# A two-layer hybrid block on one core: GpSimd's order of squares and rotation, four-step down-projections, and a shorter list ahead of the first scores

## The chip, the cores and the metric

The kernel runs on one core of a Trainium2 chip. The metric is device time in microseconds (us) of one execution, the median of several runs. The core has five engines with queues of their own, each of which works in order: TensorE (PE in the profile; its weight loads are PEld), VectorE (DVE), ScalarE (ACT), GpSimd (POOL) and SyncE (SP, which here only issues DMAs). GpSimd issues DMAs too. All DMAs run on 16 DMA engines.

## The reference

The input x is 4 x 1024 x 256 in float32. Four blocks are added to it one after the other, each on the layer norm of what stands there:

```
x = x + attention_a(norm(x));  x = x + ffn(norm(x))
x = x + attention_b(norm(x));  x = x + ffn(norm(x))
```

Both attentions have 16 heads of 64 and a full softmax over 1024 keys. Attention a makes queries, keys and values straight from the 256 columns. Attention b norms again (with scale and bias), projects down to 128 columns for queries and 128 for keys and values, projects up to heads, and rotates queries and keys: of each even and odd component e and o with the angle of the position,

```
rot = stack([e * cos - o * sin, e * sin + o * cos])
out = out @ w_out.T + residual
```

Its top-k indices are not part of the result. The ffn is 256 to 1024 and back, with a gelu.

## The kernel before, in words

All of x stays in SBUF as four tiles of 128 x 8 x 256, one a batch. Products are in float32.

*Attention.* Work goes by head pairs: for each of 4 batches 8 pairs of heads, 32 in all, which `attention` numbers g. For each head pair there are 8 steps, one for each block of 128 queries, 256 steps s in all. A step makes the scores of its queries for both heads (128 x 1024 each, `scores`, L214), their negative maximum on DVE (L224), the exponentials on ScalarE (L225), the inverted sums (`invert`), and a transpose of all probabilities on DVE within squares of 32 x 32 (`turn`, L244).

Two consecutive steps share a buffer T; here they are called a couple, numbered h. What DVE's transpose leaves undone, moving squares between groups of partitions, is done by 16 DMAs of 136 KB from T to pT (`send`, L261): SyncE issues eleven at the end of the couple's second step, GpSimd five in the step after. `weigh` multiplies the values by pT (av) in two halves, in steps 2h + 4 and 2h + 5; `divide` applies the sums (oT), and `project` multiplies by the output weights two steps later (po); ScalarE copies po to got, and GpSimd adds it to x (L292). T and pT have two buffers each, got one, the scores' PSUM three.

The order on every engine is written out by hand in `steps_with`, which is the order in the code: in step s come the inverted sums of s, the scores of s + 1 and the first exponentials, GpSimd's squares (even steps), `project` with its add, `weigh`, the second exponentials, `divide`, `turn`, SyncE's squares (odd steps), and last the pieces that are due in step s. Pieces are the preparation of a later head pair or batch; a dictionary keeps them by step, and those of one step run in the order in which they were put in.

*Preparation in layer B.* For head pair g, counted from step 8(g - 1): `qk(i, qb)` makes keys (i = 1) at -1 and 1 and queries (i = 0) at 3 and 5, for two blocks of 512 positions. It has ScalarE copy the product to `straight` (L596) and has GpSimd issue two DMAs of 128 KB that exchange even and odd partitions into `turned` (L598). One step later `rotate` runs three GpSimd operations (L603 to L605): straight times cosine, turned times sine (with the sign in the table), and the sum. Values come at 5 and 7. For a batch, `batch_b` standardizes its rows twice, adds to x on GpSimd (L551), transposes, and projects down (`down`, pc): both blocks for keys and values in step 3NT - 1 = 23 of the batch's count, both for queries in step 25. The first key product of the batch's first head pair falls in step 23 as well.

*Start.* What the first head pair of layer A needs stands in a list `first` and runs before step -1: the weight loads, standardization of both blocks of 512 rows with their statistics, transposes, two key products, two query products and four value products, in this order. For layer B the same list is worked off inside the first ffn's loop.

*ffn* runs between and after the attentions, its ends overlapped with their steps; the change leaves it alone but for the list just named.

Of the kernel before, what the change touches and what calls it, by code (L numbers as in the profile page):

```python
# [28 lines left out]
NHB = NT // HB  # L29
LAG = 4  # L30
NK = 2 * NT + 1
SENT = NG * HB * NK * SQ
POOL_DMA = 5
EPS = 1e-5
# [3 lines left out]
def hybrid_block_kernel(  # L38
# [98 lines left out]
    def standardize(dst, src, shift, rstd):  # L137
        nc.scalar.activation(dst, src, AF.Identity, scale=rstd, bias=shift)  # L138
# [24 lines left out]
    def attention(prep_batch, prep_pair, wo):  # L163
# [118 lines left out]
        def project(h):  # L282
            g, t0 = divmod(HB * h, NT)
            b, pr = pairs[g]
            po = ps_mm.tile([P, HB, D], F32, tag="mm", name="po")
            for t in range(HB):
                paired(po[:, t, :], [(oT[h][:, ts(t, P)], [wos[g]] * 2)])
            oT.pop(h)
            got = tmp.tile([P, HB, D], F32, tag="tmp", name="got")
            nc.scalar.copy(got, po)  # L290
            xd = xs[b][:, t0 : t0 + HB, :]
            nc.gpsimd.tensor_add(xd, xd, got)  # L292

        def steps_with(others):
            for k, f in others:
                pieces.setdefault(k, []).append(f)
            for s in range(-1, n + LAG + 1):
                h, part = divmod(s - LAG, HB)
                ahead = 0 <= s + 1 < n
                if 0 <= s < n:  # L300
                    invert(s)
                if ahead:
                    scores(s + 1)
                    exponentials(s + 1, 0)
                if part == 0 and 0 <= s // HB - 1 < n // HB:
                    send(s // HB - 1, nc.gpsimd, squares[len(squares) - POOL_DMA :])
                    T.pop(s // HB - 1)
                if part == 0 and 0 <= h - 1 < n // HB:
                    project(h - 1)
                if 0 <= h < n // HB:  # L310
                    weigh(h, part)
                if ahead:
                    exponentials(s + 1, 1)
                if part == 1 and 0 <= h < n // HB:
                    divide(h)
                if 0 <= s < n:
                    turn(s)
                if part == 1 and 0 <= s < n:
                    send(s // HB, nc.sync, squares[: len(squares) - POOL_DMA])
                for f in pieces.get(s, ()):  # L320
                    f()

        return first, steps_with
# [127 lines left out]
    def layer_a():  # L451
# [5 lines left out]
        def batch_a(b):  # L457
            work = []
            for qb in range(NQB):
                k = {}  # L460

                def straight(t, b=b, k=k, qb=qb):
                    if t == 0 and b == 0:
                        for i in range(TQ):
                            rows.measure(qb, i)
                        rows.finish[qb]()
                    if t == 0:
                        k["xn"] = xnp.tile([P, TQ, D], F32, tag="xn", name="xn")
                    standardize(
                        k["xn"][:, t, :], xs[b][:, qb * TQ + t, :],  # L470
                        *rows.factors(NQB * b + qb, t)[:2],
                    )

                def turned(c, b=b, k=k, qb=qb):
                    if c == 0:
                        p, tag = ((lowp, "low"), (highp, "high"))[qb]
                        hTs[b, qb] = p.tile([P, NC, QB], F32, tag=tag, name="hT")
                    transposed(hTs[b, qb], k["xn"], c)

                work += [(10 * qb + t, lambda t=t, f=straight: f(t)) for t in range(TQ)]  # L480
                work += [(10 * qb + 5 + 2 * c, lambda c=c, f=turned: f(c)) for c in range(NC)]
            return work
# [42 lines left out]
        later = [(4 + i, lambda i=i: rows.measure(2 + i // TQ, i % TQ)) for i in range(6 * TQ)]  # L525
        later += [(4 + 6 * TQ, lambda: rows.finish[2]())]
        first, steps = attention(batch_a, pair_a, wo_a)
        return first, lambda others: steps(later + others)


    def layer_b(rows):
# [4 lines left out]
        def batch_b(b):  # L536
            work = []
            for qb in range(NQB):
# [33 lines left out]
                work += [(10 * qb + t + 2, lambda t=t, f=second: f(t)) for t in range(TQ)]  # L572
                work += [(10 * qb + 7 + 2 * c, lambda c=c, f=turned: f(c)) for c in range(NC)]

                work += [(3 * NT + 1 - 2 * i, lambda i=i, f=down: f(i)) for i in range(2)]
            return work

        def pair_b(b, pr):
            made = {}

            def load():
                w = made["w"] = wp.tile([P, 3, NC, P], F32, tag="w", name="w")[:, :, 0, :]
                for i, up in enumerate((wuq, wuk, wuv)):
                    nc.gpsimd.dma_start(w[:, i], up[:, ts(pr, P)])

            def qk(i, qb):

                pq = ps_mm.tile([P, QB], F32, tag="mm", name="pq")
                paired(pq, [(made["w"][:, i, :], [cs[b, i][:, ts(qb, QB)]] * 2)])
                name = ("qT", "kT")[i]  # L590
                if qb == 0:
                    made[name] = qkp.tile([P, S], F32, tag=name, name=name)
                straight = made[name][:, ts(qb, QB)]
                turned = rp.tile([P, QB], F32, tag="turned", name="turned")
                made[i, qb] = straight, turned
                nc.scalar.mul(straight, pq, (scale_b, 1.0)[i])  # L596
                for r in range(2):
                    nc.gpsimd.dma_start(turned[r::2], straight[1 - r :: 2])  # L598

            def rotate(i, qb):  # L600

                straight, turned = made[i, qb]
                nc.gpsimd.tensor_mul(straight, straight, cos_sb[:, ts(qb, QB)])  # L603
                nc.gpsimd.tensor_mul(turned, turned, sin_sb[:, ts(qb, QB)])  # L604
                nc.gpsimd.tensor_add(straight, straight, turned)  # L605

            def values(qb):
                if qb == 0:
                    made["v"] = vp.tile([P, NT, P], F32, tag="v", name="v")
                pv = ps_mm.tile([P, TQ, P], F32, tag="mm", name="pv")  # L610
                for t in range(TQ):
                    lhsT = cs[b, 1][:, ts(qb * TQ + t, P)]
                    paired(pv[:, t, :], [(lhsT, [made["w"][:, 2, :]] * 2)])
                nc.scalar.copy(made["v"][:, ts(qb, TQ), :], pv)

            work = []
            for i in (1, 0):
                for qb in range(NQB):
                    k = 3 - 4 * i + 2 * qb
                    work += [(k, lambda i=i, qb=qb: qk(i, qb))]  # L620
                    work += [(k + 1, lambda i=i, qb=qb: rotate(i, qb))]
            work += [(5 + 2 * qb, lambda qb=qb: values(qb)) for qb in range(NQB)]
            return {name: lambda name=name: made[name] for name in ("qT", "kT", "v")}, load, work

# [21 lines left out]
def _rope_tables():  # L646
# [7 lines left out]
    sin = np.concatenate([np.sin(freqs), np.sin(freqs)], -1)[:, ::2]  # L654
    cos = np.repeat(cos.T, 2, axis=0)
    sin = np.repeat(sin.T, 2, axis=0)
    sin[0::2] *= -1.0
    return cos.astype(np.float32), sin.astype(np.float32)


# [40 lines left out]
```

## Time and profile before

| | us |
|---|---|
| three runs | 3381.72, 3386.45, 3389.66 |
| median | 3386.45 |
| profiled execution, its own time | 3386.3 |
| its span on the core | 3384.5 |
| PE busy in the span | 3253.2 (96%) |
| DVE busy | 2593.1 (77%) |
| ACT busy | 1902.1 (56%) |
| POOL busy | 1800.8 (53%) |
| first scores on PE | 27.85 |

The profile's page names groups of instructions as line, engine, operation, output<-inputs, with the count, the busy time and the mean of one, and the idle time of the engine before them with what ended it. A DMA's row on GpSimd or SyncE is the time of its issue; how long it took to land stands in a part of its own. The timeline merges neighbours of one kind ("x5") and gives start and duration. The stretches give the busy time of each engine between two times, and the share of their time that the 16 DMA engines moved data.

Layer A runs from about 28 to 1450 us, the ffn to 1750, layer B to 3150, and the second ffn to the end.

### The profile page before, as it was taken

The page shows a single profiled execution, that of the slowest core. Times are in us where ns is not written, and L with a number is a line of the kernel's source. Part 1 is how long each engine was busy: PE and PEld are TensorE (multiplying, and loading weights), DVE is VectorE, ACT ScalarE, POOL GpSimd, SP SyncE. Part 2 cuts the span into 40 slices and gives each one's busy share as a digit, 9 for nine tenths or more (in the row PEclk, how much of TensorE's full clock was granted, in tenths as well). Part 3 has the DMA queues.
Part 4 walks back from the last instruction along what each step waited for, and adds up shares of the span by engine and source line. Part 5 has one row for each costly group of instructions (what it writes and reads, how often), then busy time and mean ns, then how long its engine had stood idle before and what let it go on. Part 6 is the DMA issues. An engine that isn't in the chain of part 4 may idle for free.

```text
span 3384.5 us, 60980 instructions
## 1 busy us (share of the span) xinstructions
PE 3253.2 (96%) x20864; PEld 1679.4 (50%) x20864; DVE 2593.1 (77%) x2638; ACT 1902.1 (56%) x3667; POOL 1800.8 (53%) x2546
## 2 busy tenths in 40 slices
PE   7999999999999999999999999999999999999999
PEld 3445444544454444456554444444444444444566
DVE  6988888888888888951059998898889989999200
ACT  5566556655565555542445665566656655655332
POOL 3333334343333343330258887888788978886200
PEclk9999999999999999999999999999999999999999
DMA  7788788888887888840038888888888888888200
GB/s 211 204 210 208 205 214 212 211 208 214 210 210 206 214 214 210 210 115 3 6 105 233 227 239 226 237 246 231 224 236 243 242 225 239 243 235 228 61 19 19
DMA packets 229585, 647.36 MB, mean 191 GB/s; under 512 B 74304, under 2 KB 82496, under 8 KB 229280
## 3 DMA queue, kind: packets, MB, share of 16 engines
q1 hardware_dynamic: 143696, 400.74, 46.2%
q0 software_dynamic: 85584, 242.74, 25.2%
q8 instruction: 170, 2.79, 0.4%
q14 instruction: 135, 1.11, 0.1%
HBM read 35.00 MB, written 4.19 MB: 12 GB/s over the span
## 4 chain that ended last, share of the span: by engine, by line
PE 67%; DVE 11%; SPq 8%; DMA 6%; issue 4%; ACT 3%; POOL 1%; DVEq 0%; POOLq 0%; ACTq 0%
PE sc L214 19%; PE av L158 18%; SPq L261 8%; PE pq L158 8%; PE po L380 7%; PE ph L369 6%; DVE nmax L224 5%; DVE T L244 5%; DMA pT<-T 5%; PE po L158 4%; PE pv L158 4%; ACT p L225 1%; PE pc L158 1%; DMA turned<-qT 1%; DVE oT L275 1%
## 5 line engine op out<-in xcount | busy, mean ns | idle before, releaser
L225 ACT ACTIVATE p<-sc,nmax 128x1024 f32<-128x1024 f32 x1024 | 1143.8, 1117 | 729.5 <-DVE nmax L224 729.5
L224 DVE TENSOR_REDUCE nmax<-sc 128x1 f32<-128x1024 f32 x1024 | 1201.9, 1215 | 325.5 <-PE sc L214 324.9
L244 DVE STREAM_TRANSPOSE T<-p 128x2176 f32<-128x2176 f32 x512 | 1246.3, 2434 | 11.1 <-ACT p L233 3.9
L158 PE MATMUL av<-pT,v 128*64 128x256 f32 x8192 | 994.7, 385 | 79.4 <-DMA pT<-T 56.9
L214 PE MATMUL sc<-kT,qT 64*128 64x512 f32 x4096 | 1033.0, 617 | 7.2 <-ACT p L225 7.2
L261 POOL DMA_DIRECT2D pT<-T x1280 | 625.8, 496 | 777.9 <-issue 268.7
L158 PEld LDWEIGHTS av<-pT,v 128*64 128x64 f32 x8192 | 579.5, 137 | 542.9 <-issue 273.3
L214 PEld LDWEIGHTS sc<-kT,qT 64*128 64x128 f32 x4096 | 366.8, 187 | 483.9 <-issue 352.5
L292 POOL TENSOR_TENSOR x<-x,got 128x512 f32<-128x512 f32 x256 | 326.8, 1276 | 224.7 <-ACT got L290 220.4
L233 ACT COPY p<-total 128x128 f32<-128x128 f32 x512 | 152.0, 297 | 312.5 <-DVE total L232 312.4
L387 DVE TENSOR_TENSOR x<-x,po 128x512 f32<-128x512 f32 x32 | 21.9, 685 | 363.4 <-PE po L380 363.4
L158 PE MATMUL po<-wo,oT 128*64 128x256 f32 x2048 | 277.7, 392 | 0.4 <-DVE oT L275 0.4
L373 ACT ACTIVATE gT<-ph,b_sb 128x512 f32<-128x512 f32 x128 | 87.4, 685 | 305.4 <-PE ph L369 305.3
L158 PE MATMUL pq<-hT,w 128*64 128x512 f32 x1024 | 247.0, 605 | 5.1 <-DVE oT L275 4.0
L158 PEld LDWEIGHTS po<-wo,oT 128*64 128x64 f32 x2048 | 124.3, 136 | 230.2 <-issue 129.5
L380 PE MATMUL po<-w_sb,gT 128*128 128x256 f32 x1024 | 226.0, 381 | 6.2 <-ACT hT L147 6.2
L369 PE MATMUL ph<-hT,w_sb 128*128 128x512 f32 x512 | 228.9, 601 | 0.2 <-ACT hT L147 0.2
L380 PEld LDWEIGHTS po<-w_sb,gT 128*128 128x128 f32 x1024 | 193.5, 190 | 38.4 <-ACT hT L147 9.0
L225 ACT ACTIVATION_READ_ACCUMULATOR p<-sc,nmax 128x1 f32 x1024 | 201.4, 197 | 0.0
L355 POOL TENSOR_TENSOR x<-x,b_sb 128x256 f32<-128x256 f32 x64 | 44.5, 727 | 276.4 <-ACT xn L138 276.4
L604 POOL TENSOR_TENSOR turned<-turned,sin_sb 128x512 f32<-128x512 f32 x128 | 162.3, 1268 | 0.0
L369 PEld LDWEIGHTS ph<-hT,w_sb 128*128 128x128 f32 x512 | 97.0, 192 | 117.1 <-issue 111.3
(88 smaller groups left out, 2188.8 us busy)
## 6 DMA issues: line engine op xcount, KB each, us to landing
pT<-T SPq DMA_DIRECT2D x2816, 136.0 KB, 4.2
pT<-T POOLq DMA_DIRECT2D x1280, 136.0 KB, 4.7
turned<-kT POOLq DMA_DIRECT2D x128, 128.0 KB, 2.7
turned<-qT POOLq DMA_DIRECT2D x128, 128.0 KB, 3.0
w<-in_wqkv_a POOLq DMA_DIRECT2D x96, 128.0 KB, 4.9
wo<-in_wo_a POOLq DMA_DIRECT2D x32, 128.0 KB, 4.4
wo<-in_wo_b POOLq DMA_DIRECT2D x32, 128.0 KB, 3.4
out<-x SPq DMA_DIRECT2D x16, 256.0 KB, 2.1
```

Of the source, the lines that this page charges most:

```text
L158: nc.tensor.matmul(out[ts(j, DH)], lhsT[:, ts(j, DH)], rhs[j], start=(first and i == 0), stop=(last and i == len(parts) - 1),)
L214: nc.tensor.matmul(sc[s, j][:, ts(m, 512)], qT()[rows, ts(qs, P)], kT()[rows, ts(m, 512)], start=True, stop=True,)
L224: nc.vector.tensor_reduce(nmax, sc[s, j], AX.X, ALU.max, negate=True)
L225: nc.scalar.activation(probs[s][:, ts(j, NT)].rearrange("p k c i -> p (k c i)"), sc.pop((s, j)), AF.Exp, bias=nmax, accum_out=total[s][:, ...
L233: nc.scalar.copy(probs[s][:, 2 * NT].rearrange("p (j c) i -> p j (c i)", j=2), t.unsqueeze(2).to_broadcast([P, 2, DH]),)
L244: nc.vector.transpose(T[h][:, :, q, :, :].rearrange("p c k i -> p k c i"), probs.pop(s))
L261: engine.dma_start(pT[h][ts(c, SQ), a], T[h][ts(a, SQ), c])
L292: nc.gpsimd.tensor_add(xd, xd, got)
L369: nc.tensor.matmul(ph, w1_sb[:, c, ts(f, P)], hT[n][:, c, :], start=(c == 0), stop=(c == NC - 1),)
L373: nc.scalar.activation(gT[n][:, f, :], ph, AF.Gelu, bias=b1_sb[:, f : f + 1])
L380: nc.tensor.matmul(po[n][:, t % 2, :], gT[n][:, f, ts(t, P)], w2_sb[:, f, :], start=(f == 0), stop=(f == NF - 1),)
L604: nc.gpsimd.tensor_mul(turned, turned, sin_sb[:, ts(qb, QB)])
```

## The change

It has three parts.

*GpSimd's order in layer B.* `project` no longer adds to x; it returns the add, and `steps_with` calls it after the pieces of the step. A second list of pieces, at s + LATE = s + 0.5, follows the add. The rotation is cut in two: part 0 (at k + 1) multiplies the straight rows by the sine into `other` and exchanges even and odd partitions of that product by DMA; part 1 (at k + 1.5) multiplies by the cosine and adds. The exchange moves from `qk` in the odd step to the even step; its sine table has the sign in the other rows.

*Down-projections.* The four `down` of a batch fall in steps 23, 24, 26 and 28 of the batch's count, keys and values first.

*Start of layer A.* The list is put in a new order: statistics of block 0, its standardization, statistics of block 1, an Exp of one column on ScalarE (`ready`), transposes of block 0, keys of block 0, standardization of block 1 (now on VectorE) and its transposes, keys of block 1, queries of block 0. The queries of block 1 become a piece of step -1 and the values pieces of steps 0 and 1.

```diff
+LATE = 0.5
             xd = xs[b][:, t0 : t0 + HB, :]
-            nc.gpsimd.tensor_add(xd, xd, got)
+            return lambda: nc.gpsimd.tensor_add(xd, xd, got)
...
+                add = None
                 if part == 0 and 0 <= h - 1 < n // HB:
-                    project(h - 1)
+                    add = project(h - 1)
...
                 for f in pieces.get(s, ()):
+                    f()
+                if add:
+                    add()
+                for f in pieces.get(s + LATE, ()):
                     f()
...
-                    if t == 0 and b == 0:
-                        for i in range(TQ):
-                            rows.measure(qb, i)
-                        rows.finish[qb]()
...
+                    if b == 0 and qb == 1:
+                        nc.vector.tensor_scalar(dst, src, rstd, shift, op0=ALU.mult, op1=ALU.add)
+                    else:
+                        standardize(dst, src, shift, rstd)
...
+        loads, xn, pair = first[:2], first[2:14], first[14:]
+
+        def measured(qb):
+            for t in range(TQ):
+                rows.measure(qb, t)
+            rows.finish[qb]()
+
+        def ready():
+
+            nc.scalar.activation(small.tile([P, 1], F32, tag="nmax", name="ready"), eps, AF.Exp)
+
+
+        first = loads + [lambda: measured(0)] + xn[:4] + [lambda: measured(1), ready] + xn[4:6] + pair[:1]
+        first += xn[6:] + pair[1:3]
+        later += [((-1, 0, 0, 1, 1)[i], f) for i, f in enumerate(pair[3:])]
...
-                work += [(3 * NT + 1 - 2 * i, lambda i=i, f=down: f(i)) for i in range(2)]
+                work += [(3 * NT - 1 + 3 * (1 - i) + qb * (2 - i), lambda i=i, f=down: f(i)) for i in (1, 0)]
...
-                straight = made[name][:, ts(qb, QB)]
-                turned = rp.tile([P, QB], F32, tag="turned", name="turned")
-                made[i, qb] = straight, turned
-                nc.scalar.mul(straight, pq, (scale_b, 1.0)[i])
-                for r in range(2):
-                    nc.gpsimd.dma_start(turned[r::2], straight[1 - r :: 2])
-
-            def rotate(i, qb):
-
-                straight, turned = made[i, qb]
-                nc.gpsimd.tensor_mul(straight, straight, cos_sb[:, ts(qb, QB)])
-                nc.gpsimd.tensor_mul(turned, turned, sin_sb[:, ts(qb, QB)])
-                nc.gpsimd.tensor_add(straight, straight, turned)
+                nc.scalar.mul(made[name][:, ts(qb, QB)], pq, (scale_b, 1.0)[i])
+
+            def rotate(i, qb, part):
+
+                dst = made[("qT", "kT")[i]][:, ts(qb, QB)]
+                if part == 0:
+                    other = rp.tile([P, QB], F32, tag="turned", name="other")
+                    nc.gpsimd.tensor_mul(other, dst, sin_sb[:, ts(qb, QB)])
+                    made[i, qb] = rp.tile([P, QB], F32, tag="turned", name="turned")
+                    for r in range(2):
+                        nc.gpsimd.dma_start(made[i, qb][r::2], other[1 - r :: 2])
+                else:
+                    nc.gpsimd.tensor_mul(dst, dst, cos_sb[:, ts(qb, QB)])
+                    nc.gpsimd.tensor_add(dst, dst, made[i, qb])
...
-                    work += [(k + 1, lambda i=i, qb=qb: rotate(i, qb))]
+                    work += [
+                        (k + 1 + LATE * m, lambda i=i, qb=qb, m=m: rotate(i, qb, m)) for m in range(2)
+                    ]
...
-    sin[0::2] *= -1.0
+    sin[1::2] *= -1.0
```

More of the change, by code (lines that the diff above doesn't have):

```diff
@@ L462, in straight @@
                 def straight(t, b=b, k=k, qb=qb):
[L463 to L466 removed]
                     if t == 0:
                         k["xn"] = xnp.tile([P, TQ, D], F32, tag="xn", name="xn")
[L469 to L472, printed above, removed]
+                    dst, src = k["xn"][:, t, :], xs[b][:, qb * TQ + t, :]
+                    shift, rstd = rows.factors(NQB * b + qb, t)[:2]
+                    if b == 0 and qb == 1:
+                        nc.vector.tensor_scalar(dst, src, rstd, shift, op0=ALU.mult, op1=ALU.add)
+                    else:
+                        standardize(dst, src, shift, rstd)
                 def turned(c, b=b, k=k, qb=qb):
```

## The prediction

> **What bounds the kernel now.** I read the page's engine table first, then the stretches, then who waits for whom, then single couples of steps. TensorE is busy 3253.2 of 3384.5 us, so no more than 131 us of idle time can be won. The stretches say where that idle time lies (columns: stretch, its length, busy PE, PEld, DVE, ACT and POOL with counts, granted clock, DMA share, GB/s; the first row is layer A, the second layer B).
>
> ```profile
> PE 3253.2 (96%) x20864; PEld 1679.4 (50%) x20864; DVE 2593.1 (77%) x2638; ACT 1902.1 (56%) x3667; POOL 1800.8 (53%) x2546
> ...
> 800.00:1200.00 400.00, 399.55 (x2870) 199.45 (x2866) 346.14 (x320) 239.15 (x475) 156.38 (x250) 1.00 0.82 210
> ...
> 2000.00:2400.00 400.00, 377.29 (x2530) 183.84 (x2532) 352.54 (x325) 246.62 (x479) 334.16 (x445) 1.00 0.88 235
> ```
>
> Layer A is TensorE from end to end (0.45 us idle in 400). Layer B idles 22.7 in 400, some 80 us over its 1400, with the 16 DMA engines at 0.88. The waits of 2000 to 2800 us name the one cause that matters on PE:
>
> ```profile
> PE av L158 <- DMA pT<-T: 29.2, 25, 2.4
> ...
> PE av L158 <- DMA turned<-qT: 4.7, 4, 1.7
> ```
>
> So weighing by the values waits for the transposed squares to land, about 1.2 us each time, once in three couples. A couple is two steps; its squares leave when its second transpose on DVE ends (call it T), and the product that needs them starts about 12 us later. Here is one couple with T = 2363.01, GpSimd first (start, duration), then the DMA share us by us from T - 1.
>
> ```profile
> 2362.35 1.13 POOL L598 DMA_DIRECT2D turned<-kT  x2 [2.56 <-ACT kT L596]
> 2363.70 2.43 POOL L261 DMA_DIRECT2D pT<-T  x5 [0.22 <-issue]
> 2366.34 1.27 POOL L292 TENSOR_TENSOR x<-x,got 128x512 f32<-128x512 f32 x1 [0.21 <-ACT got L290]
> 2367.58 1.26 POOL L603 TENSOR_TENSOR kT<-kT,cos_sb 128x512 f32<-128x512 f32 x1
> 2368.81 1.26 POOL L604 TENSOR_TENSOR turned<-turned,sin_sb 128x512 f32<-128x512 f32 x1
> 2370.15 1.28 POOL L605 TENSOR_TENSOR kT<-kT,turned 128x512 f32<-128x512 f32 x1
> ```
>
> ```profile
> 2362.01:2363.01 1.00, 1.00 (x6) 0.21 (x4) 1.00 (x2) 0.71 (x2) 0.66 (x2) 1.00 0.00 0
> 2363.01:2364.01 1.00, 1.00 (x10) 0.58 (x10) 0.74 (x3) 0.30 (x1) 0.78 (x2) 1.00 0.32 131
> 2364.01:2365.01 1.00, 1.00 (x14) 0.64 (x12) 1.00 (x2) 0.43 (x1) 1.00 (x3) 1.00 0.93 270
> ...
> 2368.01:2369.01 1.00, 1.00 (x11) 0.65 (x11) 1.00 (x3) 0.30 (x1) 1.00 (x2) 1.00 1.03 287
> 2369.01:2370.01 1.00, 1.00 (x10) 0.58 (x8) 1.00 (x2) 0.77 (x1) 1.00 (x1) 1.00 1.00 309
> ```
>
> The DMA engines are empty just before T, begin with the exchange of rows for the rotation (issued at T - 0.66), and are full from T + 1 to T + 9. Lining up 108 couples of layer B (all but its first and last few) by T gives these means. SyncE issues its eleven squares by T + 9.0 and the last lands at 11.98. GpSimd's five start at T + 1.4 and land at 9.1. The product starts at 12.96. In none of the 108 do GpSimd's squares land last. In 52 the exchange goes out before T - 0.5 and the last square lands at 11.56; in the other 56 (GpSimd's squares start at T + 2.0) it lands at 12.37.
>
> The delay closes a loop. The product of couple h delays the scores behind it in PE's order; the DVE work of three more steps follows, until the T of couple h + 3; then the landing. It took 3 x 11.01 = 33 us a round, the mean distance of two T being 11.01. A landing that comes d later costs at most d/3 a couple, over 128 couples 43 d.
>
> **The change, part by part.**
>
> *The rotation on GpSimd (layer B, 31 of 32 head pairs, 124 couples).* Per couple it removes and adds nothing in count: three elementwise operations of 1.27 us, two DMAs of 128 KB at 0.55 us of issue, five squares of 0.49. The order changes. Before: exchange (in the odd step, waiting for ScalarE), squares, x add, cosine, sine, sum. After, all in the even step: squares, sine product, exchange of the product, x add, cosine, sum. Squares start at T + 0.69, as in the undisturbed couple above, and end at T + 3.1; sine product until 4.4; exchange issued 4.5 to 5.6; x add and cosine (2.55 us) until 8.2; the sum waits for the landing.
>
> GpSimd's squares gain 1.4 - 0.7 = 0.7 us in the mean. They had about 2.9 us of room (9.1 against 11.98), so that alone moves no landing; it can only fill the engines a little earlier: SyncE alone offers 136 KB each 0.6 us, 227 GB/s, some 83% of the 270 that the full rows show, so 1.3 us of lateness in 56 couples wastes 0.2 us each.
>
> The exchange loses its place. It leaves a time in which DMA is idle (0.00 and 0.32 in the rows) and goes to T + 4.5, where the share is 1.0. 256 KB at 270 GB/s are 0.95 us of all engines. From below: nothing, if the exchange cost as much in its old place. From above: 0.95. Layer A, which has no exchange, lands at 11.4 in couples without a weight load, and layer B with an early exchange at 11.5 without one, so the old place cost 0.1 to 0.15 and the new one costs the rest: up to 0.8 in the 52 couples, about nothing in the 56 that already had it behind T. The mean is 0.48 x 0.8 - 0.52 x 0.2 = 0.28; with weight loads that collide with it as well (most of layer A's couples with one land at 12.4 to 13.2) I take 0.35. Cost: 43 x 0.35 = 15; a fifth of the couples have PE work enough to hide it (the preparation of a batch), so 12 us. Bounds: d = -0.2 gives -7, d = 0.8 gives +28.
>
> Here a rule of the Trainium skill speaks against the change. DMA: Bandwidth & Descriptors, "Issuing engines are not separate DMA queues", says that transfers of all issuing engines run on the same 16 engines and interleave, and that another issuing engine saves issue time alone. The rows agree: SyncE's squares share with GpSimd's. The same page ("Anatomy of one DMA", a fit of 2.0 us plus bytes over 436 GB/s) would land the exchange's 128 KB in 2.3 us. Its own row has 2.7 and 3.0, in the idle time, and the row of GpSimd's squares, in the full time, 4.7:
>
> ```profile
> pT<-T POOLq DMA_DIRECT2D x1280, 136.0 KB, 4.7
> turned<-kT POOLq DMA_DIRECT2D x128, 128.0 KB, 2.7
> turned<-qT POOLq DMA_DIRECT2D x128, 128.0 KB, 3.0
> ```
>
> I take 4.7. GpSimd's own round is then 2.45 + 1.27 + 1.1 + 4.7 + 1.28 = 10.8 us against a couple's 11.0 (by the page 8.4: ample). It just fits, and the next squares stay at T + 0.7. Nothing else is late: a head pair's keys and first half of queries are complete by the end of step 5 of its count and read by scores in step 7, the second half by the end of step 7 and read in step 11. The x add moves from T + 3.3 to T + 5.6 and releases the one buffer that ScalarE's next copy needs two steps later; that cover is about 4 us. Loads of weights follow the exchange in GpSimd's queue and are needed more than a step later.
>
> *Down-projections.* Three batches have them inside the steps (the first is in the feed-forward part). The same 16 products of four groups are spread: two bursts of 3.65 us become four pieces of 1.83, in couples that follow each other. PE work is the same. What is saved is idle time after the bursts: DVE waited 4.11 us for scores behind the first one, and the head pairs that hold the bursts have 0.4, 4.2 and 2.3 us of PE idle; bound 0 to 6, I take 3. New: the key product of the new batch follows its only piece and waits for ScalarE's copy (0.58, ScalarE was idle before it) and the semaphores, 0.7 to 1.9, times three; I take 1 each. Together 0.
>
> *Start.* Key product of block 0 moves ahead of block 1's transposes, one query product and all values products move behind the first scores, VectorE standardizes block 1, and the Exp table is loaded early.
>
> ```profile
> 16.29 8.10 PE L158 MATMUL pq<-hT,w 128*64 128x512 f32 x32
> 24.21 3.71 PE L158 MATMUL pv<-w,hT 128*64 128x128 f32 x64
> 27.85 2.84 PE L214 MATMUL sc<-kT,qT 64*128 64x512 f32 x10
> 32.38 2.25 PE L214 MATMUL sc<-kT,qT 64*128 64x512 f32 x8 [1.70 <-ACT p L225]
> ```
>
> ScalarE ends block 0 at 10.0, then the square root (0.3), the table (1.28), one Exp (0.3), two copies (0.59 each): 13.1. Keys of block 0 on PE from 12.6 to 14.9 (8.10/4 = 2.03 each, the first slower), eight transposes to 16.5, keys of block 1 to 18.9, queries to 20.9, copy, first scores at 21.6: 6.2 us earlier. The deferred 2.03 + 3.71 = 5.7 us lie on PE, which before had 1.70 + 1.44 + 2.40 = 5.5 us of idle time between 27.85 and 54.4; with about 2 us of it left unused the gain is 4 us (0.5 if none of it covers, 6.2 if all). The page ScalarE: Activation LUTs, "What ACT_TABLE_LOAD costs", has about 2.7 us for the load with its drain; with that the first scores come 1.4 later and 2.6 remain. The ten rows of the trace have 1.283, and I use that.
>
> Sum against the profiled 3386.3 (span 3384.5 and 1.8 around it; the median of the three runs is 3386.45, the same): + 12 + 0 - 4 = 3394 us.
>
> **The rivals.**
>
> *GpSimd closes its round* (15%). If the exchange lands 5.3 us after its issue instead of 4.7, the round is 11.4 against 11.0, squares start later each couple until the exchange slides out of the full time again. Half of 124 x 0.4 = 25 us on top of a landing some 0.1 later: about 3412. For it: a head pair brings four weight DMAs (2.4 us) too, and the preparation of a batch eight adds of 0.74. Against: two of the waits overlap them.
>
> *The other side: squares on time* (25%). The exchange costs what it did, because the engines owe the same bytes each round, and the 56 late couples land at 11.9 instead of 12.37: mean d = -0.2, -7 us; the bursts' idle time goes for 3; the start gives 4.5. 3386.3 - 14.5 = 3372. It decides where d falls below 4/34 = 0.12. For it: at 0.88 the engines are not full, and a fifth of the couples has GpSimd's squares over 1.5 us late. Against: those couples' products wait little more than others (19.6 us in 25 couples, 44.4 in 83: 0.25 us each, 6 in all), and SyncE's squares are always last.
>
> *Nothing measurable* (20%): d about 0.1 and the start cancel, 3386. For it: all terms are a third of a percent or less.
>
> **How the numbers follow.** The likeliest, a later landing, has 40% and its own range 3388 to 3404. About 0.2%, 6.8 us, is what a measurement of this kernel can tell from no change: of that 40, 5 fall within it. Slower: 35 + 15 = 50, faster 25, same 20 + 5 = 25. The range reaches to both other cases, 3371 to 3412; below it lies part of the squares-on-time case, above it part of the closed round.
>
> **What would show it.** The first scores at 21 to 23 us. In layer B the exchange issued 4 to 6 us after T and landing 4.5 to 5 later; GpSimd's squares at T + 0.7 in nearly all couples; SyncE's last square at 12.3 instead of 11.98 in the mean; PE's waits for squares longer than the 56.9 us that the whole program has now, layer B longer by about 12. Pieces of 1.83 us in place of 3.65. I am wrong if the landing comes no later than before, or if the sum on GpSimd runs past the next T and its squares start over 1.5 us late.

## The result and the profile after

The changed kernel takes 3465.15 us (median; 3463.93 to 3469.07), against 3386.47 before (3381.72 to 3389.66): ratio 1.0236, 95% interval 1.0218 to 1.0253, so some 79 us slower. The prediction was 3394, its range 3371 to 3412: the direction was right, the size wrong, and the time lies outside the range. The profiled execution has a span of 3462.9 us (3384.5 before). A trace is of one execution, which can lie up to 10 us from the median of its kernel, so differences of traces and of medians do not quite agree.

The page's engine table of the changed kernel, its row of the product that weighs the values (busy time, mean ns, idle time before it and what ended most of that), and its DMA rows (KB each, us to landing):

```profile
PE 3273.6 (95%) x20864; PEld 1681.8 (49%) x20864; DVE 2600.0 (75%) x2642; ACT 1899.9 (55%) x3664; POOL 1817.2 (52%) x2546
...
L159 PE MATMUL av<-pT,v 128*64 128x256 f32 x8192 | 1011.7, 390 | 135.0 <-DMA pT<-T 109.0
...
pT<-T SPq DMA_DIRECT2D x2816, 136.0 KB, 4.4
pT<-T POOLq DMA_DIRECT2D x1280, 136.0 KB, 4.4
turned<-other POOLq DMA_DIRECT2D x256, 128.0 KB, 4.7
```

The waits of the product for squares grew from 56.9 to 109.0 us, and the exchange takes 4.7 us to land where it took 2.7 and 3.0. The stretches, with the columns of the prediction, put the loss in one place:

```profile
800.00:1200.00 400.00, 398.82 (x2860) 198.74 (x2858) 346.74 (x321) 239.29 (x474) 157.49 (x249) 1.00 0.83 211
2000.00:2400.00 400.00, 360.76 (x2394) 174.28 (x2388) 337.60 (x310) 235.28 (x458) 322.98 (x424) 0.98 0.86 223
```

Layer A is as before; in layer B PE idles 39 us of 400 (22.7 before). By the transposes, from the first T to the last T (T is the end of a couple's second transpose on DVE), layer A takes 1434.3 us (1431.0 before), and layer B 1477.0 (1395.1): the 82 us are there. The first scores come at 21.61 (27.85 before), and all of layer B's loss sits on top of that small gain.

The 82 us are not all waiting. These rows run from layer B's first T to its last, before and after (the granted clock is the number ahead of the DMA share):

```profile
1743.12:3138.27 1395.15, 1307.16 (x8706) 641.64 (x8707) 1248.66 (x1182) 855.12 (x1659) 1147.53 (x1524) 0.99 0.87 234
...
1740.38:3217.40 1477.02, 1330.89 (x8708) 646.97 (x8709) 1253.95 (x1182) 854.87 (x1659) 1161.03 (x1524) 0.98 0.85 221
```

PE idles 58 us more (146.1 against 88.0) and is busy 24 us more with the same products. In the trace the granted clock stands at 0.5 in 17 stretches of 3.4 or 6.8 us, 68 us together (6 stretches, 20 us, before); half of the difference is 24 us. Each of these stretches, before and after, has at least 1.6 us of idle PE in the 3.4 us ahead of it, and of PE's pauses over 2 us there are now 25 (7 before). So long waits cost twice here; this is read from the order in time alone, no run changes the clock by itself. One case, the first half of a product behind a wait, then its second half, and the row of the clock, which halves 2.3 us into that wait:

```profile
2164.56 3.68 PE L159 MATMUL av<-pT,v 128*64 128x256 f32 x16 [4.18 <-DMA pT<-T]
...
2170.72 1.95 PE L159 MATMUL av<-pT,v 128*64 128x256 f32 x16
```

```profile
2162.65:2169.48 6.83, 4.92 (x20) 2.71 (x22) 2.49 (x2) 1.43 (x4) 6.29 (x10) 0.50 0.98 254
```

Who waits for whom in 2000 to 2800 us, changed kernel (us in total, times, longest):

```profile
PE av L159 <- DMA pT<-T: 56.8, 32, 4.2
...
POOL kT L624 <- DMA turned<-other: 50.6, 27, 3.6
...
POOL qT L624 <- DMA turned<-other: 35.2, 18, 3.3
...
DVE T L245 <- DMA pT<-T: 14.2, 14, 2.6
```

The first is the wait of before, doubled (29.2). The next two are new: GpSimd's sum waits for the exchange. In the last, VectorE's transpose waits until squares have left the buffer T (1.3 before), a second way in which lateness costs. One couple shows the first two. T is 2405.41; GpSimd first (start, duration), then the DMA share (the last column but one) in single us:

```profile
2405.58 1.27 POOL L624 TENSOR_TENSOR kT<-kT,turned 128x512 f32<-128x512 f32 x1 [0.90 <-DMA turned<-other]
2406.80 2.49 POOL L262 DMA_DIRECT2D pT<-T  x5
2409.30 1.28 POOL L618 TENSOR_TENSOR other<-qT,sin_sb 128x512 f32<-128x512 f32 x1
2410.88 1.15 POOL L621 DMA_DIRECT2D turned<-other  x2 [0.29 <-POOL other L618]
...
2416.36 1.26 POOL L624 TENSOR_TENSOR qT<-qT,turned 128x512 f32<-128x512 f32 x1 [0.18 <-DMA turned<-other]
```

```profile
2405.40:2406.40 1.00, 1.00 (x10) 0.58 (x10) 0.74 (x3) 0.30 (x1) 0.82 (x1) 1.00 0.00 0
...
2410.40:2411.40 1.00, 1.00 (x11) 0.64 (x12) 1.00 (x3) 0.30 (x1) 0.70 (x2) 1.00 1.02 235
...
2416.40:2417.40 1.00, 0.73 (x8) 0.20 (x4) 1.00 (x2) 0.00 (x0) 1.00 (x1) 1.00 0.97 257
```

The previous sum ends at T + 1.4, so GpSimd's squares start late; the exchange goes out at T + 5.5 into full engines (T + 6.3 in the mean of the 108 couples that the experiments line up); and the engines are still full at T + 12, where the product starts to idle.

### The profile page after: what moved, and what is told of

The parts are those of the page before. It is cut to its first block, busy times and chain, and to the rows that moved or that the text cites. A ratio compares the mean times of both kernels' runs of the same rounds, so it can differ in the third digit from the quotient of the medians.

```text
span 3462.9 us, 60831 instructions
## 1 busy us (share of the span) xinstructions
PE 3273.6 (95%) x20864; PEld 1681.8 (49%) x20864; DVE 2600.0 (75%) x2642; ACT 1899.9 (55%) x3664; POOL 1817.2 (52%) x2546
## 4 chain that ended last, share of the span: by engine, by line
PE 66%; DVE 13%; DMA 7%; SPq 6%; issue 5%; ACT 2%; POOL 1%; DVEq 0%; POOLq 0%
PE sc L215 19%; PE av L159 18%; PE pq L159 7%; PE po L386 7%; DMA pT<-T 6%; SPq L262 6%; PE ph L375 6%; DVE T L245 6%; DVE nmax L225 5%; PE po L159 4%; PE pv L159 4%; DVE oT L276 1%; PE pc L159 1%; ACT p L226 1%; PE tr L145 0%
## 5 line engine op out<-in xcount | busy, mean ns | idle before, releaser
L159 PE MATMUL av<-pT,v 128*64 128x256 f32 x8192 | 1011.7, 390 | 135.0 <-DMA pT<-T 109.0
L159 PEld LDWEIGHTS av<-pT,v 128*64 128x64 f32 x8192 | 587.7, 139 | 606.1 <-issue 276.1
L621 POOL DMA_DIRECT2D turned<-other x256 | 145.6, 571 | 41.2 <-POOL other L618 37.7
```

The lines of the kernel that those rows point to most:

```text
L159: nc.tensor.matmul(out[ts(j, DH)], lhsT[:, ts(j, DH)], rhs[j], start=(first and i == 0), stop=(last and i == len(parts) - 1),)
L621: nc.gpsimd.dma_start(made[i, qb][r::2], other[1 - r :: 2])
```

## The experiments

Two theories were set against each other at first. A: GpSimd's round no longer closes, because the sum waits for an exchange that lands late. B: the exchange takes DMA time from the squares, because it moved from a time in which the engines are empty to one in which they are full. The table lines up the same 108 couples of layer B by T, as the prediction did: when the last of SyncE's squares lands, when the product starts, when GpSimd's squares start (us after T), and the mean distance of two T.

| kernel | time, us | ratio to before | last square lands | product starts | GpSimd's squares start | couple |
|---|---|---|---|---|---|---|
| before | 3386.5 | | 11.98 | 12.96 | 1.40 | 11.01 |
| after | 3465.2 | 1.0236 | 12.79 | 14.00 | 2.12 | 11.70 |
| rotation alone | 3475.1 | 1.0265 | 12.77 | 14.22 | 1.89 | 11.81 |
| start alone | 3379.8 | 0.9984 | 11.93 | 12.95 | 1.43 | 11.00 |
| start and down-projections | 3386.2 | 1.0003 | 11.86 | 12.90 | 1.28 | 11.10 |
| after, exchange not waited for | 3456.3 | 1.0212 | 12.78 | 13.79 | 0.82 | 11.55 |
| after, no exchange | 3376.4 | 0.9969 | 11.69 | 12.74 | 0.61 | 10.98 |
| after, half the exchange | 3415.0 | 1.0089 | 12.25 | 13.29 | 0.68 | 11.30 |
| after, exchange behind the sum | 3411.8 | 1.0069 | 12.09 | 13.20 | 0.84 | 11.23 |

### Each part by itself

The rotation's new order alone (the first of the change's three parts; of its diff these lines and the two halves of `rotate`):

```diff
-                    project(h - 1)
+                    add = project(h - 1)
...
+                if add:
+                    add()
+                for f in pieces.get(s + LATE, ()):
+                    f()
...
-                    work += [(k + 1, lambda i=i, qb=qb: rotate(i, qb))]
+                    work += [
+                        (k + 1 + LATE * m, lambda i=i, qb=qb, m=m: rotate(i, qb, m)) for m in range(2)
+                    ]
```

> Only the new order on GpSimd in layer B (squares, sine product, exchange, x add, cosine, sum); start and down-projections as before. The changed kernel took 78.7 us more than before, and its trace puts first scores 6.3 us earlier and the start of layer B's scores 2.7 us earlier, so all of the loss and more lies in layer B. If the order on GpSimd alone makes the loss: 3386 + 79 + 3 = 3468 us, within 6. If the spread down-projections share in it: 3440 or less.

Measured: 3475.1 us, ratio 1.0265 (1.0242 to 1.0288). The whole loss, and 10 more, is in this part. The 10 are not more waiting: between layer B's first and last T, PE idles 142.2 us (146.1 in the changed kernel) but is busy 1344.7 (1330.9), with 24 stretches at half clock instead of 17.

The new start alone (the third part):

```diff
+        first = loads + [lambda: measured(0)] + xn[:4] + [lambda: measured(1), ready] + xn[4:6] + pair[:1]
+        first += xn[6:] + pair[1:3]
+        later += [((-1, 0, 0, 1, 1)[i], f) for i, f in enumerate(pair[3:])]
```

> Only the new start of layer A. From the trace of the changed kernel, where layer B's first scores came 2.7 us earlier: 3383.7 us, ratio 0.9992. By the prediction's step: 4 us less, 3382.5. If the shift of the first scores were kept whole: 6.3 us less.

Measured: 3379.79 us, ratio 0.9984 (0.9975 to 0.9992). It is the fastest kernel here that computes all.

The new start and the down-projections:

```diff
-                work += [(3 * NT + 1 - 2 * i, lambda i=i, f=down: f(i)) for i in range(2)]
+                work += [(3 * NT - 1 + 3 * (1 - i) + qb * (2 - i), lambda i=i, f=down: f(i)) for i in (1, 0)]
```

> Start and spread down-projections, GpSimd's order as before. If spreading is worth nothing, as the prediction had it: the same as the new start alone, 3383.7 us. If it saves the idle time behind the bursts: 3 to 6 us less, 3378 to 3381. If the wait of the key product for its copy costs as much as the bursts did: 3386 to 3388.

Measured: 3386.24 us, ratio 1.0003 (0.9991 to 1.0015): 6.5 slower than the start alone. The waits on PE of 1750 to 3150 us in this kernel name what was bought:

```profile
PE pc L158 <- ACT got L290: 4.5, 9, 0.6
...
PE pq L158 <- ACT c L582: 2.1, 3, 0.7
```

The second is the key product's wait that the prediction had, 0.7 each. The first it had not: a single piece (pc) comes to stand behind the output product (po), and the two PSUM buffers of the kind are then both in use until ScalarE has copied po to got: nine waits of 0.5 us. Together 6.6; that this is the 6.5 is in part chance, since with the other waits PE idles 5.3 us more there than with the start alone (85.6 against 80.3), and in the traces PE is also 5.4 us longer busy in layer B (1317.8 against 1312.4, granted clock 0.986 and 0.989).

### The exchange: waiting for it, or having it there

The changed kernel with the exchange still issued, but the sum reads `other` instead of its result (so the rotation isn't computed):

```diff
-                    made[i, qb] = rp.tile([P, QB], F32, tag="turned", name="turned")
+                    turned = rp.tile([P, QB], F32, tag="turned", name="turned")
                     for r in range(2):
-                        nc.gpsimd.dma_start(made[i, qb][r::2], other[1 - r :: 2])
+                        nc.gpsimd.dma_start(turned[r::2], other[1 - r :: 2])
+                    made[i, qb] = other
```

> The changed kernel, but the sum of the rotation takes the sine product itself in place of its exchanged rows (so queries and keys are rotated wrongly); the exchange is still issued at the same place, with the same bytes, and nothing waits for it. Theory A, GpSimd closes its round (squares, sine product, exchange, landing, sum, next squares): without the wait for the landing the squares start on time again, and most of the 79 us goes: 3384 to 3412 us, with GpSimd's squares at 0.7 us after the second transpose and the last square landing at 12.2 to 12.6. Theory B, the exchange displaced into the time in which the DMA engines are full: nothing changes in that, so 3445 to 3470 us.

Measured: 3456.28 us, ratio 1.0212 (1.0187 to 1.0236). GpSimd's squares are back at T + 0.82, its waits for the exchange are gone, and the time is 9 us better (3447 to 3458 in its executions, against 3464 to 3469): theory A falls as the main cause. In the same 800 us the waits that matter are as they were:

```profile
DVE nmax L225 <- PE sc L215: 112.0, 91, 4.3
...
PE av L159 <- DMA pT<-T: 52.3, 33, 3.7
...
DVE T L245 <- DMA pT<-T: 14.5, 12, 2.1
```

The same kernel without the two DMAs of the exchange (rotation not computed):

```diff
-                    made[i, qb] = rp.tile([P, QB], F32, tag="turned", name="turned")
-                    for r in range(2):
-                        nc.gpsimd.dma_start(made[i, qb][r::2], other[1 - r :: 2])
+                    made[i, qb] = other
```

> The changed kernel without the exchange of rows: the sum takes the sine product as it is (queries and keys are rotated wrongly), and the 256 KB a couple are not moved. The run without the wait took 3456 with GpSimd's squares on time and the last square landing at 12.78. Displaced exchange: the last square lands at 11.2 to 11.6 and the time is 3340 to 3372 us, the whole loss and part of the waits of before gone. Something else in the new order (the add behind the pieces, the sine product ahead, the down-projections): 3440 us or more.

Measured: 3376.43 us, ratio 0.9969 (0.9958 to 0.998). The squares land at 11.69, and layer B's stretch is back at PE 378.34:

```profile
2000.00:2400.00 400.00, 378.34 (x2536) 181.60 (x2534) 354.79 (x327) 248.00 (x483) 296.20 (x369) 1.00 0.83 211
```

So 80 us hang on 256 KB a couple in the new place. In the old place they cost about 10 (3386.2 with the new start and the down-projections, 3376.4 without exchange; these two differ in GpSimd's order too, and the old order without its exchange was not run). Squares are waited for without any exchange too: 26.3 us on PE in 2000 to 2800 us, against 29.2 before. That is the floor which the expectation had set too low.

### Bytes or place

The kernel of the unread exchange, with half of it (one DMA of 128 KB):

```diff
-                    for r in range(2):
-                        nc.gpsimd.dma_start(turned[r::2], other[1 - r :: 2])
+                    nc.gpsimd.dma_start(turned[0::2], other[1::2])
```

> As the run in which the sum waits for nothing, with one of the two DMAs of the exchange (128 KB a couple instead of 256, same place, rotation wrong as there). The run without it took 3376, the one with both 3456. In proportion: 3416, landing 12.2. A threshold near a landing of 12: below 3400.

Measured: 3415.03 us, ratio 1.0089 (1.0061 to 1.0117), as in proportion: 3376, 3415 and 3456 for 0, 128 and 256 KB. That is 40 us for each 128 KB a couple.

The exchange issued behind the sum, at about T + 8.5 and unread, with the same instructions and bytes:

```diff
                     nc.gpsimd.tensor_add(dst, dst, made[i, qb])
+                    turned = rp.tile([P, QB], F32, tag="turned", name="turned")
+                    for r in range(2):
+                        nc.gpsimd.dma_start(turned[r::2], made[i, qb][1 - r :: 2])
```

> The same kernel as the run in which the sum waits for nothing, same instructions and bytes, but the exchange is issued at the end of GpSimd's work of a couple, after the sum (about 8.5 us after the second transpose in place of 4.6), so that it moves when the squares are nearly through. If the place in the DMA engines' full time is the cause: landing at 11.4 to 12.0 and 3360 to 3400 us. If it is the number of bytes alone, wherever they lie: 3445 to 3460.

Measured: 3411.83 us, ratio 1.0069 (1.0052 to 1.0086): between the two. Of the 80 us, 44 go by moving the DMAs 3 to 4 us later (T + 8.5 in the mean, against T + 5.0), when fewer squares are left to come behind them.

Four DMAs (512 KB) in the new place, unread:

```diff
-                    for r in range(2):
+                    for r in (0, 1, 0, 1):
```

> As the run in which the sum waits for nothing, but the exchange is issued twice (512 KB a couple, the second copy over the first; nothing waits for it, rotation wrong as there). Displaced exchange: landing at about 13.6 and 60 to 100 us more than that run, 3515 to 3555. If the bytes are not the cause: about 3456, at most 15 more for GpSimd's issue time.

Measured: 3711.0 us in one run, far above. It says nothing more on the amount, since another limit sets in: GpSimd is overrun, its squares start at T + 6.7, and the scores wait for its rotated queries (waits on PE, 2000 to 2800 us):

```profile
PE sc L215 <- POOL qT L625: 87.5, 14, 8.1
```

The start alone, with the exchange in its old place but issued by ScalarE, directly behind its copy:

```diff
-                    nc.gpsimd.dma_start(turned[r::2], straight[1 - r :: 2])
+                    nc.scalar.dma_start(turned[r::2], straight[1 - r :: 2])
```

> Before, with the new start of layer A and one edit: the exchange of rows is issued by ScalarE right behind the copy that it reads, and not by GpSimd. It leaves at about 0.9 us before the second transpose ends, and GpSimd's squares are never behind it. If the place of the exchange decides: squares at 0.7, landing near 11.5, 3335 to 3370 us, faster than before by 0.4 to 1.4%. If ScalarE's issue time (about 1.2 us a couple) holds up its exponentials: 3385 to 3410.

Measured: 3412.2 us, ratio 1.0074 (1.0058 to 1.0089), 32 slower than the start alone, and outside both expectations. GpSimd's squares do start at T + 0.77; but SyncE, whose last issue ended at T + 9.0, now needs until T + 9.66, and its last square lands at 12.16. Why ScalarE's issues slow SyncE's was not followed up.

### What lateness alone costs

The start alone with four, and with six, of the sixteen squares on GpSimd instead of five (and twelve and ten on SyncE):

```diff
-POOL_DMA = 5
+POOL_DMA = 4
```

> Before with the new start, and one constant changed: GpSimd sends four squares of a couple and SyncE twelve. No byte is added and nothing on GpSimd is moved; the last square of SyncE should land some 0.5 to 0.8 us later in layer B, at 12.4 to 12.7 (layer A, where TensorE sets the pace, has 1.8 us of room). This is a dial for the landing alone. By the prediction's step, a delay d costs at most a third of it a couple: 7 to 11 us, 3387 to 3391. By the slope of the runs so far (about 0.55 us a couple for 0.8 us of landing, once it is past 12): 3420 to 3440.

> The same dial the other way: six squares on GpSimd, ten on SyncE; landing at 11.2 to 11.5. A third of it a couple: 3370 to 3374. If the time is flat below a landing of about 12, as the run without the exchange suggests: 3376 to 3382. If GpSimd's sixth square is held behind its rotation: slower, 3385 or more.

Measured: 3385.62 (1.0008; 0.9994 to 1.0021) and 3391.11 (1.0019; 1.0003 to 1.0034). Neither moved the landing as meant (12.03 and 11.90; 11.93 with five), so neither says what lateness costs. Five is the best of the three.

One, and two, DMAs of four bytes ahead of SyncE's squares in layer B, with the start alone:

```diff
+            if engine is nc.sync and wo is wo_b:
+                for i in range(1):
+                    engine.dma_start(spare[0:1, i : i + 1], eps[0:1])
             for a, c in which:
                 engine.dma_start(pT[h][ts(c, SQ), a], T[h][ts(a, SQ), c])
```

> The new start alone, with one DMA of four bytes, into a spare tile, issued by SyncE ahead of its eleven squares in layer B: it makes the squares late without moving data. An issue on SyncE takes 0.59 + 0.04 us in the chain of before, so the last square should land some 0.6 us later. If lateness is paid over two couples (a product holds the scores of the second step after it, whose maxima stand ahead of the transpose that ends the couple two further on), a couple grows by 0.3 and the time by 0.3 x 124 x 0.8 = 30 us over the 3380 of the new start alone: 3410. If it is paid over three couples, as predicted: 0.2 a couple, 20 us, 3400. If lateness of landing is not what costs, but the displaced bytes are: 3380 to 3385.

> As before, with two such DMAs of four bytes: landing some 1.25 us later. Two couples: 0.6 a couple, 60 to 70 us, 3440 to 3450. Three couples: 0.4 a couple, 40 to 45 us, 3420 to 3425. Bytes and not lateness: 3380 to 3390.

Measured: 3422.67 us (1.0110; 1.0079 to 1.0140) and 3422.07 (1.0110; 1.0074 to 1.0147). The timeline with one of them (T = 2414.40) shows that it doesn't go out with the squares: it waits for no transpose and leaves 2.6 us ahead of them.

```profile
2411.91 0.60 SPq L264 DMA_DIRECT2D spare<-eps  x1
2411.97 2.43 DVE L246 STREAM_TRANSPOSE T<-p 128x2176 f32<-128x2176 f32 x1
...
2414.48 8.09 SPq L266 DMA_DIRECT2D pT<-T  x11
```

With one the squares land at 12.35, 0.42 later than with the start alone, with no data moved to speak of, and a couple takes 11.22 instead of 11.00: 0.22, a half and not a third. With two, SyncE's last issue ends at T + 9.39 instead of 9.13, yet the product starts no later (13.38 and 13.36) and the time is the same; when their squares land the trace does not tell. The times fit no theory: 3423 lies above all that was expected of one, and 3422 is what three couples were expected to give for two. Between the traces of the start alone and of one DMA, 24.9 us are in layer B (T to T), and 12 in layer A, which has none of these DMAs. So only the length of the couple speaks for a half here.

### The suspected round, shortened

Lateness of a product may come back through VectorE's queue two couples later (the lines are in the next section). To shorten that path, VectorE's transpose is moved ahead of the multiplication by the inverted sums, in the kernel with the start alone and in the changed one:

```diff
-                if part == 1 and 0 <= h < n // HB:
-                    divide(h)
                 if 0 <= s < n:
                     turn(s)
+                if part == 1 and 0 <= h < n // HB:
+                    divide(h)
```

> The new start alone, with VectorE's multiplication by the inverted sums moved behind the transpose of its step: VectorE's work is the same, the transpose ends 0.34 to 0.42 us earlier. If the round over two couples sets the time in about half of the couples, 0.17 x 124 x 0.5 = 10 us are gained: 3370. If the loop runs over three couples or VectorE's place in it is not tight: within 4 of 3380. If the later release of the product's PSUM buffer costs more: 3385 to 3395.

> The changed kernel with the same move on VectorE. If the round over two couples sets the time in nearly all couples of layer B, it gains 0.17 to 0.21 x 124 = 21 to 26 us: 3440 to 3445. If not: 3460 to 3470.

Measured: 3567.16 us (1.0539; 1.0515 to 1.0562) and 3604.49 (1.0645; 1.0618 to 1.0672), far above the 3385 to 3395 and the 3460 to 3470 that were expected at worst, and the lines below show why. The multiplication also frees the PSUM buffer of the product (av). Freed 2.4 us later, it leaves one buffer for the pieces behind it. Layer A, kernel with the start alone and this move:

```profile
898.79 1.89 PE L158 MATMUL pq<-hT,w 128*64 128x512 f32 x8
...
901.38 1.09 PE L158 MATMUL pv<-w,hT 128*64 128x128 f32 x16 [0.70 <-ACT qT L502]
901.75 0.39 DVE L275 TENSOR_TENSOR oT<-av,pT 128x256 f32<-128x256 f32 x1
...
902.40 1.99 PE L214 MATMUL sc<-kT,qT 64*128 64x512 f32 x8
...
904.42 2.36 DVE L224 TENSOR_REDUCE nmax<-sc 128x1 f32<-128x1024 f32 x2 [2.22 <-PE sc L214]
```

The piece pv waits for ScalarE to empty pq's buffer, the scores stand behind it, and DVE waits 2.22 us for them. Whether the shorter path to T is worth anything can't be read from a kernel with this wait in it; in layer B of the changed kernel it came out level (1480.7 us, T to T, against 1477.0).

## Why the prediction was wrong

*The size of d: wrong.* The step "The mean is 0.48 x 0.8 - 0.52 x 0.2 = 0.28; ... I take 0.35" failed. The landing moved from 11.98 to 12.79, by 0.81: the upper bound. The prediction took the exchange of the 56 couples in which it went out after T - 0.5 to be as dear already as at T + 4.5, and it is not: of all that the exchange cost in its old place, early or late, the runs find 0.2 to 0.3 us of landing (11.86 to 11.98, against 11.69 without it, in the new order). In the new place it costs 1.09 (12.78). 256 KB at the 270 GB/s of the full rows are 0.97 us of all engines (the prediction's 0.95 counts 1000 bytes to a KB): what was put ahead of the last squares in full engines delayed them by about its whole transfer time. Half of it costs half (0.56), and 3 to 4 us later it costs 0.40.

*The conversion: wrong.* "A landing that comes d later costs at most d/3 a couple" rests on a round of three couples. Between the kernels without, with half and with the whole unread exchange, 1.09 us of landing became 0.57 us a couple; with the four-byte DMA 0.42 became 0.22. Both are 0.52; it is no constant, since the exchange behind the sum has 0.40 and 0.25, and the exchange on ScalarE 0.23 and 0.27. The trace has a round of two couples that the prediction passed over. These lines of the changed kernel begin with a late product and end with the T of the couple shown above, 2405.41:

```profile
2396.47 1.95 PE L159 MATMUL av<-pT,v 128*64 128x256 f32 x16 [1.92 <-DMA pT<-T]
2398.34 1.99 PE L215 MATMUL sc<-kT,qT 64*128 64x512 f32 x8
...
2400.36 2.35 DVE L225 TENSOR_REDUCE nmax<-sc 128x1 f32<-128x1024 f32 x2 [1.45 <-PE sc L215]
...
2402.64 0.41 DVE L276 TENSOR_TENSOR oT<-av,pT 128x256 f32<-128x256 f32 x1
2402.97 2.44 DVE L245 STREAM_TRANSPOSE T<-p 128x2176 f32<-128x2176 f32 x1
```

The first half of couple h's product, in step 2h + 4, delays the scores of step 2h + 6 right behind it; their maxima stand in VectorE's queue ahead of the transpose of step 2h + 5; and that is the second transpose of couple h + 2, not h + 3. From the start of the product to that T it takes 8.94 us here, and this stretch is nearly rigid: 8.88 to 9.05 in 89 of the 108 couples before and in 74 after, so a late product makes that T late by as much. Where it takes over 9.5 us after the change (24 couples), a stretch at half clock lies in it in 14.

A delay that goes round once in two couples costs half of itself a couple. With the measured d and a half for the third, the prediction's own sum is 0.81 x 64 x 0.8 = 41 us in place of 12. The traces have 54 for layer B between the kernel with start and down-projections alone and the one that adds the new order with its exchange unread (1405.7 and 1459.8), and the medians 70, so more is in it than this. The path from the product to T is shown by the couples, but that the round of two sets the pace is argued from them and the slopes: by the trace a product waits for its squares in 51 of the 108 couples after and 38 before, and the attempt to shorten the round failed for another reason. (The round of three that the prediction added up to 33 us proves nothing: from one T to that of three couples on is three couples whatever lies between.)

*The clock: not in the sum.* The prediction counts waits alone and leaves PE's speed as it was. Of the 82 us by which layer B grew, 24 are products that take longer, at half clock behind the long waits. Between no exchange and the whole unread one it is 12 of 65 (PE busy 1312.2 and 1324.6 us, T to T), so about a fifth of the 0.52 too.

*GpSimd's round: wrong, and small.* "It just fits, and the next squares stay at T + 0.7": they start at T + 2.12, and later than T + 1.5 in 68 of the 108 couples (25 before), though the exchange lands in the 4.7 us that were taken. A sum of 10.8 against 11.0 had no room for the four weight DMAs of 0.55 that a head pair brings (three of them are in the couple of the timeline after the exchange), nor for the 0.3 between the product and its first DMA. This was the rival with 15%, but it costs 9 us, since GpSimd's squares still land first (9.59 against 12.79). With the landing unchanged, couples are still 0.15 longer (11.70 against 11.55); of the 17 us that this makes in layer B, 6 are PE's longer busy time (1330.9 against 1324.6), and the rest stays open.

*Down-projections: wrong by 6.5.* The three waits of 0.7 are the lower end of what was predicted. The saving of 3 wasn't found, and the wait for a PSUM buffer that the piece now has (4.5) was put at nothing.

*Start: right.* First scores at 21.61, worked out as 21.6 with the 1.283 us of the trace for the table load, behind which ScalarE goes on within 0.02 us (the Trainium skill's page ScalarE: Activation LUTs, "What ACT_TABLE_LOAD costs", has about 2.7 us with the drain, which would have made it 23.0; this trace shows the load alone), and a gain of 4 to 5 us: predicted 4, measured 4.7 (by the interval 3 to 8).

Put together from the medians of the runs: start -5, down-projections +6.5, the moved exchange +70, the wait for it +9. These are steps from one kernel to the next, so their sum of 81 is no proof of them (the 79 measured has a median of before that lies 2 us higher). The parts are not strictly additive: the rotation alone cost 90.

*The rivals.* "Squares on time" counted on the engines owing the same bytes each round. They do, but the share of a round is the wrong measure: the same bytes cost 80 us at T + 5, 35 at T + 8.5 and about 10 around T.

## What to carry to other kernels

Look at the DMA share from the event that starts the critical transfers, microsecond by microsecond, and treat its empty part as a resource: a transfer in it is nearly free (about 10 us here), and the same transfer put ahead of the last critical one in the full part made that one later by about its whole transfer time, each round (80 us in all). Compare the busy time of the same products too: behind the longer waits TensorE ran at half clock, which made 24 of the 82 us in layer B. Before dividing a delay by the length of a loop, walk the queues in order and stop at the first thing that can be late again; here a maximum queued ahead of a transpose makes it two couples and not three. And a round that was to fit by 0.2 of 11 us did not.

## What was not expected

- Four-byte DMAs on SyncE, issued in its idle time, made its squares land 0.42 us later, and slowed a layer that has none by 12 us. No cause was found.
- ScalarE issuing 256 KB a couple slowed SyncE's eleven issues from T + 9.0 to T + 9.66.
- VectorE's 0.4 us multiplication, moved behind a transpose of 2.4, cost 187 us in all, 124 of it in layer A, through a PSUM buffer that the waits of before name only as weight loads waiting for oT (pv 51.6 us, pq 30.7) and as 8.0 us of PE ahead of pq.
